# Moving the elu's positive part to the ScalarE and layer 3's bias to the heads' results in a four-layer graph attention kernel

## The chip, the cores and the metric

The kernel runs on one core of one Trainium2 chip. A core has a matrix engine (TensorE, in the profile PE; its weight loads are a row of their own, PEld), a vector engine (VectorE, DVE), an engine for activation functions (ScalarE, ACT), a general engine (GpSimd, POOL) and a queue for transfers (SyncE, SP). Each engine works through its own list of instructions in order, and they wait for each other through semaphores. The metric is the device time of one launch in microseconds (us). Before the change it is 3154.01 us, the median of 3 runs (3153.35 to 3154.1).

## The reference

The input is `x`, 16 graphs of 1024 nodes with 256 features, and `adj`, their adjacency. Four layers follow, each in the same frame: a layer norm and a relu, then a graph attention whose result is added to `x`.

```python
# --- layers 1 and 2: an elu follows the attention ---
h = jnp.maximum(_layernorm(x, axis=-1), 0.0)
x = x + _L1_gnn_ref(h, adj, ...)        # ... return jax.nn.elu(h_prime)
# (layer 0 has no elu; layer 2 is like layer 1 with other scores)

# --- layer 3: four heads of 64 features, a bias, a relu, a layer norm for each head ---
h = jnp.einsum('bnd,hde->bhne', nodes_embed, W)
# ... weight, leaky_relu, softmax -> attention
dst = jnp.einsum('bhij,bhje->bhie', attention, h) + bias[None, :, None, :]
out = jax.nn.relu(dst) + h
mu = out.mean(axis=-1, keepdims=True)
var = out.var(axis=-1, keepdims=True)
out = (out - mu) / jnp.sqrt(var + EPS) * ln_gamma[...] + ln_beta[...]
```

Two identities matter here. The elu is `max(v, 0) + min(exp(v), 1) - 1`; the kernel collects the two `-1` of layers 1 and 2 in a constant that is added with `beta`. And since the attention weights of a row sum to one, a bias may be added to the values before the attention or to its result after it.

## The kernel before

The kernel is written in a tile framework. The framework sets the semaphores and also decides, from the program's text, the order in which the instructions stand in each engine's list. Two graphs at a time are worked on as two interleaved streams, each with its own two PSUM accumulators (`acc0`, `acc1`).

The projection of a pair of node tiles, and the eviction of it in layer 3:

```python
    def project(b, l, xb, pair, evict):
        # ... bn_stats / bn_aggr per tile (DVE), rstd by pow (POOL), centered = max(x - mean, 0) (DVE)
        turned = psum.tile([P, NK, 2 * P], F32, name="misc")
        # ... four transposes on PE
        hT = wide.tile([P, NK, 2 * P], F32, name="hT", bufs=3)
        nc.scalar.copy(hT, turned)
        for n in range(2):
            projected = accumulator(b)[:, : D + EXT[l]]
            for k in range(NK):
                nc.tensor.matmul(projected, hT[:, k, ts(n, P)], W[l][:, k, :], ...)
            evict(2 * pair + n, projected, rstd[:, n : n + 1])

            def evict3(i, projected, rstd):
                nc.scalar.activation(ex[:, i, :], projected[:, D:], AF.Exp, scale=rstd)
                nc.scalar.mul(h3[:, i, :], projected[:, :D], rstd)

                q = ex[:, i, :H].unsqueeze(2)
                values = V3[:, i, :, :E]
                nc.gpsimd.tensor_add(
                    values, h3[:, i, :].rearrange("p (h e) -> p h e", h=H),
                    bias.rearrange("p (h e) -> p h e", h=H),
                )
                nc.gpsimd.tensor_mul(values, values, q.to_broadcast([P, H, E]))
                nc.gpsimd.tensor_copy(V3[:, i, :, E:], q)
                nc.gpsimd.tensor_add(xb[:, i, :], xb[:, i, :], beta)
```

The attention of layers 0 to 2: eight matmuls for each of eight node tiles, then the finish of the tile, which for layers 1 and 2 is the elu. The next layer's projection of a pair starts when both its tiles are finished.

```python
    def add_elu(xi, acc):
        inv = small.tile([P, 1], F32, name="inv")
        inverse(inv, acc[:, D : D + 1])               # max with a tiny number, reciprocal: two DVE instructions
        below = work.tile([P, D], F32, name="below", bufs=2)
        nc.scalar.activation(below, acc[:, :D], AF.Exp, scale=inv)
        above = work.tile([P, D], F32, name="above", bufs=2)
        nc.vector.tensor_scalar(above, acc[:, :D], inv, 0.0, op0=ALU.mult, op1=ALU.max)
        nc.vector.scalar_tensor_tensor(above, below, 1.0, above, op0=ALU.min, op1=ALU.add)
        nc.gpsimd.tensor_add(xi, xi, above)

            for i in range(NI):
                # ... eight matmuls into acc
                finish(i, acc)
                if l == 2:
                    next(testing)                     # one ACT pass (Square) over a tile of adj
```

Layer 3's heads: the scaled results of a head are collected in `y`, centred and scaled.

```python
        def center(h):
            yh = y[:, :, h, :]
            head = ts(h, E)
            nc.vector.scalar_tensor_tensor(yh, yh, 0.0, h3[:, :, head], op0=ALU.max, op1=ALU.add)
            mean = small.tile([P, NI], F32, name="mean")
            nc.vector.tensor_reduce(mean, yh, AX.X, ALU.add)
            nc.vector.tensor_scalar_mul(mean, mean, 1.0 / E)
            nc.vector.tensor_sub(yh, yh, mean.unsqueeze(2).to_broadcast(shape))
            # ... square (ACT), var (DVE), rstd by pow (POOL)

        def rescale(yh, head, rstd):
            nc.vector.tensor_mul(yh, yh, rstd.unsqueeze(2).to_broadcast(shape))
            nc.gpsimd.tensor_mul(yh, yh, gamma[:, head].unsqueeze(1).to_broadcast(shape))
            nc.gpsimd.tensor_add(yh, yh, xb[:, :, head])
```

## Time and profile before

| what | before |
|---|---|
| time, median of 3 runs | 3154.01 us |
| span of the profiled execution | 3152.2 us |
| PE busy | 3005.1 us (95%) |
| DVE busy | 2377.5 us (75%) |
| POOL busy | 1077.7 us (34%) |
| ACT busy | 732.0 us (23%) |
| mean granted clock of TensorE | 0.987 of full |

The page gives the busy time of each engine and, in its fourth part, the chain of work that ended last: starting at the last instruction, it goes back from each instruction to the one that released it. An engine can be busy most of the time and still not set the end; the chain tells which one does. The groups of instructions give, for one source line, how many there were, how long one took, and how long the engine stood idle just before them. The waits list the same idle times by who waited for whom. The timeline lists instructions in order of time, which is needed where the question is what happens at one place in the program; the pattern repeats about every 383 us, once for each pair of graphs.

### The profile page before, as it was taken

To read this page: it belongs to the slowest core of one execution; us is meant where nothing else is said; L and a number is where in the kernel's file an instruction comes from. 1 tells how busy PE (TensorE), PEld (TensorE's weight loads), DVE (VectorE), ACT (ScalarE), POOL (GpSimd) and SP (SyncE) were. 2 spreads that over 40 slices of the span, in tenths; PEclk is the share of its full clock that TensorE was granted. 3 is DMA by queue.
4 is the path that set the end of the run, shared out by engine and by line. 5 is a ranking of instruction groups with operands and counts; after the bars stand their busy time and mean duration, and the time that the engine had idled before them with its cause. 6 is when DMAs were issued, how large, how long until landed. Compare 5 with 4: busy or idle time off the path is not lost.

```text
span 3152.2 us, 35624 instructions
## 1 busy us (share of the span) xinstructions
PE 3005.1 (95%) x12678; PEld 2071.0 (66%) x12678; DVE 2377.5 (75%) x5243; ACT 732.0 (23%) x1729; POOL 1077.7 (34%) x1460
## 2 busy tenths in 40 slices
PE   7899999999999999999999999999999999999987
PEld 5676766668666686666767567666775657766662
DVE  5677678786878768787687876878768787787756
ACT  1221223113131221312213122231222212222130
POOL 1332424233252342423425224252333423233242
PEclk9999999999999999999999999999999999999998
DMA  5512212122120221302303022021221221001010
GB/s 112 65 16 27 47 21 43 25 27 51 17 61 7 54 29 13 64 4 54 41 2 66 8 54 34 14 54 14 51 30 21 47 27 40 14 14 27 1 28 15
DMA packets 116872, 105.53 MB, mean 33 GB/s; under 512 B 73680, under 2 KB 91216, under 8 KB 116688
## 3 DMA queue, kind: packets, MB, share of 16 engines
q0 software_dynamic: 44256, 81.80, 15.9%
q1 hardware_dynamic: 72432, 21.37, 3.6%
q8 instruction: 103, 1.69, 0.2%
q14 instruction: 81, 0.66, 0.1%
HBM read 153.49 MB, written 33.55 MB: 59 GB/s over the span
## 4 chain that ended last, share of the span: by engine, by line
PE 81%; DVE 10%; POOL 4%; ACT 2%; issue 1%; DMA 1%; ACTq 0%; POOLq 0%; SPq 0%; DVEq 0%
PE acc L383 36%; PE acc L489 27%; PE acc L271 12%; DVE weights L292 5%; PE misc L264 3%; PE row L288 2%; POOL rstd L239 1%; PE misc L504 1%; DVE stats L251 1%; DVE above L317 1%; ACT below L315 1%; POOL out_dram L520 1%; POOL x_b L319 1%; DMA weights<-in_L_gnn_a_src_dram 1%; DVE centered L256 1%
## 5 line engine op out<-in xcount | busy, mean ns | idle before, releaser
L383 PE MATMUL acc<-V,weights 128*128 128x257 f32 x6144 | 1435.2, 383 | 23.1 <-DVE weights L292 11.0
L383 PEld LDWEIGHTS acc<-V,weights 128*128 128x128 f32 x6144 | 1149.2, 191 | 325.2 <-issue 90.3
L489 PE MATMUL acc<-weights,V 128*65 128x512 f32 x2048 | 957.9, 592 | 1.5 <-POOL V L358 1.5
L239 POOL TENSOR_TENSOR rstd<-rstd,minus_half 128x2 f32<-128x2 f32 (+1 forms) x320 | 295.2, 924 | 1054.0 <-DVE rstd L238 1040.8
L292 DVE SCALAR_TENSOR_TENSOR weights<-row,ex,mask 128x1024 f32<-128x1024 f32 x512 | 626.9, 1275 | 18.7 <-PE acc L489 9.3
L271 PE MATMUL acc<-W,hT 128*128 128x259 f32 (+1 forms) x2048 | 536.9, 401 | 59.4 <-DVE above L317 25.6
L271 PEld LDWEIGHTS acc<-W,hT 128*128 128x128 f32 x2048 | 389.8, 197 | 195.8 <-issue 70.8
L292 DVE SCALAR_TENSOR_TENSOR weights<-row,V,mask 128x1024 f32<-128x1024 f32 x384 | 475.1, 1275 | 45.7 <-PE row L288 45.7
L489 PEld LDWEIGHTS acc<-weights,V 128*65 128x65 f32 x2048 | 272.7, 138 | 353.5 <-issue 313.5
L319 POOL TENSOR_TENSOR x_b<-x_b,above 128x256 f32<-128x256 f32 x256 | 188.2, 738 | 687.6 <-DVE above L318 609.5
L315 ACT ACTIVATE below<-acc,inv 128x256 f32<-128x256 f32 x256 | 120.6, 473 | 821.3 <-DVE inv L308 571.3
L251 DVE BATCH_NORM_STATS2 stats<-x_b 128x6 f32<-128x256 f32 x512 | 209.1, 415 | 109.6 <-POOL x_b L319 101.5
L266 ACT COPY hT<-misc 128x512 f32<-128x512 f32 x256 | 149.5, 585 | 476.8 <-PE misc L264 476.3
L256 DVE TENSOR_SCALAR centered<-x_b,mv 128x256 f32<-128x256 f32 x512 | 216.6, 425 | 4.6
L264 PE MATMUL misc<-ident,centered 128*128 128x128 f32 x1024 | 166.8, 278 | 37.9 <-DVE centered L256 28.7
L264 PEld LDWEIGHTS misc<-ident,centered 128*128 128x128 f32 x1024 | 127.0, 142 | 114.9 <-DVE centered L256 48.4
L333 ACT ACTIVATE V<-acc,rstd 128x3 f32<-128x3 f32 x384 | 98.9, 262 | 423.7 <-PE acc L271 422.1
L337 DVE TENSOR_SCALAR V<-acc,rstd,V 128x256 f32<-128x256 f32 x256 | 134.5, 538 | 75.0 <-ACT V L333 73.4
L317 DVE TENSOR_SCALAR above<-acc,inv 128x256 f32<-128x256 f32 x256 | 122.2, 480 | 69.2 <-ACT below L315 68.7
L499 ACT COPY sums<-acc 65x512 f32<-65x512 f32 x128 | 74.5, 582 | 378.8 <-PE acc L489 378.8
L307 DVE TENSOR_SCALAR inv<-acc 128x1 f32<-128x1 f32 x256 | 39.2, 153 | 146.1 <-PE acc L383 143.9
L132 ACT ACTIVATE adj_i<-adj_i,minus_half 128x1024 bf16<-128x1024 bf16 x128 | 145.8, 1139 | 0.0
(68 smaller groups left out, 1946.7 us busy)
## 6 DMA issues: line engine op xcount, KB each, us to landing
adj_i<-in_adj_dram POOLq DMA_DIRECT2D x128, 256.0 KB, 3.9
narrow<-in_adj_dram POOLq DMA_DIRECT2D x64, 256.0 KB, 8.8
out_dram<-y POOLq DMA_DIRECT2D x32, 512.0 KB, 4.0
x_b<-in_x_dram POOLq DMA_DIRECT2D x14, 1024.0 KB, 7.1
x_b<-in_x_dram SPq DMA_DIRECT2D x2, 1024.0 KB, 7.4
mask<-narrow SPq DMA_TRANSPOSE x64, 3.8
W<-in_L_gnn_W_dram SPq DMA_DIRECT2D x3, 256.0 KB, 11.4
weights<-in_L_gnn_a_dram SPq DMA_DIRECT2D x3, 256.0 KB, 12.8
```

The costliest lines, as they stand in the source:

```text
L239: nc.gpsimd.tensor_tensor(r, r, minus_half.to_broadcast([P, n]), op=ALU.pow)
L251: nc.vector.bn_stats(stats, xb[:, 2 * pair + n, :])
L256: nc.vector.tensor_scalar(centered[:, n, :], xb[:, 2 * pair + n, :], mv[:, n, 0:1], 0.0, op0=ALU.subtract, op1=ALU.max,)
L264: nc.tensor.transpose(turned[:, k, ts(n, P)], centered[:, n, ts(k, P)], ident)
L266: nc.scalar.copy(hT, turned)
L271: nc.tensor.matmul(projected, hT[:, k, ts(n, P)], W[l][:, k, :], start=(k == 0), stop=(k == NK - 1),)
L292: nc.vector.scalar_tensor_tensor(w, r, c(j), masks[b][:, j // 2, :, j % 2], op0=op, op1=ALU.mult)
L315: nc.scalar.activation(below, acc[:, :D], AF.Exp, scale=inv)
L317: nc.vector.tensor_scalar(above, acc[:, :D], inv, 0.0, op0=ALU.mult, op1=ALU.max)
L319: nc.gpsimd.tensor_add(xi, xi, above)
L383: nc.tensor.matmul(accs[i], weights[j][:, ts(i, P)], V[:, j, : D + 1], start=(j == 0), stop=(j == NI - 1),)
L489: nc.tensor.matmul(accT, V3[:, j, h, :], weights[h * NI + j][:, ts(g, HALF)], start=(j == 0), stop=(j == NI - 1),)
```

## The change

The change has two parts. In `add_elu` the positive part of the elu is computed by ACT, as a relu of the accumulator scaled by `inv`, right after the exponential of the same accumulator, and no longer by DVE. This takes an instruction from the busier of the two engines that read the accumulator. In layer 3 the bias is no longer added to the values in `evict3`, where it cost one addition for each node tile; it is added to a head's results at the start of `center`, one addition for each head over all eight node tiles. Both additions stand on POOL.

```diff
         below = work.tile([P, D], F32, name="below", bufs=2)
         nc.scalar.activation(below, acc[:, :D], AF.Exp, scale=inv)
         above = work.tile([P, D], F32, name="above", bufs=2)
-        nc.vector.tensor_scalar(above, acc[:, :D], inv, 0.0, op0=ALU.mult, op1=ALU.max)
+        nc.scalar.activation(above, acc[:, :D], AF.Relu, scale=inv)
         nc.vector.scalar_tensor_tensor(above, below, 1.0, above, op0=ALU.min, op1=ALU.add)
         nc.gpsimd.tensor_add(xi, xi, above)
@@
                 nc.scalar.mul(h3[:, i, :], projected[:, :D], rstd)
-
                 q = ex[:, i, :H].unsqueeze(2)
-                values = V3[:, i, :, :E]
-                nc.gpsimd.tensor_add(
-                    values, h3[:, i, :].rearrange("p (h e) -> p h e", h=H),
-                    bias.rearrange("p (h e) -> p h e", h=H),
-                )
-                nc.gpsimd.tensor_mul(values, values, q.to_broadcast([P, H, E]))
+                nc.gpsimd.tensor_mul(
+                    V3[:, i, :, :E], h3[:, i, :].rearrange("p (h e) -> p h e", h=H),
+                    q.to_broadcast([P, H, E]),
+                )
                 nc.gpsimd.tensor_copy(V3[:, i, :, E:], q)
@@
             yh = y[:, :, h, :]
             head = ts(h, E)
+            nc.gpsimd.tensor_add(yh, yh, bias[:, head].unsqueeze(1).to_broadcast(shape))
             nc.vector.scalar_tensor_tensor(yh, yh, 0.0, h3[:, :, head], op0=ALU.max, op1=ALU.add)
```

## The prediction

> **What bounds the kernel now.** I read the busy shares first, then the chain of work that ended last, then the groups, to see what the change touches. These are lines of the page:

> ```profile
> PE 3005.1 (95%) x12678; PEld 2071.0 (66%) x12678; DVE 2377.5 (75%) x5243; ACT 732.0 (23%) x1729; POOL 1077.7 (34%) x1460
> ...
> PE 81%; DVE 10%; POOL 4%; ACT 2%; issue 1%; DMA 1%; ACTq 0%; POOLq 0%; SPq 0%; DVEq 0%
> ```

> PE is busy for 95% of the span and carries 81% of the chain. The change adds no matmul and takes none away. So it can only move the time in which PE stands still or runs slowly. How much is that? I took the busy time by stretches, without the first 300 us and the end:

> ```profile
> 300.00:3000.00 2700.00, 2624.31 (x11136) 1813.19 (x11135) 2072.71 (x4551) 641.36 (x1518) 938.68 (x1267) 0.99 0.18 31
> ```

> In these 2700 us PE is idle for 75.7 us. If all of it went, the kernel would be 2.4% faster; that is about the ceiling, and the change touches a small share of it. Next, the groups that the change removes, copies or delays:

> ```profile
> L317 DVE TENSOR_SCALAR above<-acc,inv 128x256 f32<-128x256 f32 x256 | 122.2, 480 | 69.2 <-ACT below L315 68.7
> L315 ACT ACTIVATE below<-acc,inv 128x256 f32<-128x256 f32 x256 | 120.6, 473 | 821.3 <-DVE inv L308 571.3 <-PE acc L383 149.7 <-DVE inv L307 57.2
> ...
> L358 POOL TENSOR_TENSOR V<-h,bias 128x256 f32<-128x256 f32 x128 | 93.6, 732 | 2.5 <-ACT h L354 2.1
> L463 POOL TENSOR_TENSOR y<-y,gamma 128x512 f32<-128x512 f32 x64 | 81.5, 1274 | 74.2 <-DVE inv L308 36.8 <-DVE y L462 25.2 <-DVE inv L307 6.4
> ```

> And from the waits, those in which PE stands behind the elu or behind the next layer's input:

> ```profile
> PE misc L264 <- DVE centered L256: 28.7, 27, 3.4
> PE acc L271 <- DVE above L317: 25.6, 12, 2.9
> ...
> PE acc L383 <- DVE above L317: 7.7, 17, 1.2
> ```

> So PE waits 33.3 us in all for an accumulator that the positive part still reads. The largest of these waits is 2.9 us and comes back in every period of 383 us. The timeline of one shows where it comes from:

> ```profile
> 930.02 1.55 POOL L520 DMA_DIRECT2D out_dram<-y  x2 [0.30 <-POOL y L464]
> ...
> 931.59 0.73 POOL L319 TENSOR_TENSOR x_b<-x_b,above 128x256 f32<-128x256 f32 x1
> ...
> 932.36 0.43 DVE L251 BATCH_NORM_STATS2 stats<-x_b 128x6 f32<-128x256 f32 x1 [0.53 <-POOL x_b L319]
> ...
> 933.49 0.16 DVE L308 RECIPROCAL inv<-inv 128x1 f32<-128x1 f32 x1
> ...
> 933.77 0.47 ACT L315 ACTIVATE below<-acc,inv 128x256 f32<-128x256 f32 x1 [2.92 <-DVE inv L308]
> ...
> 934.28 0.48 DVE L317 TENSOR_SCALAR above<-acc,inv 128x256 f32<-128x256 f32 x1 [0.62 <-ACT below L315]
> ...
> 934.91 0.51 PE L271 MATMUL acc<-W,hT 128*128 128x268 f32 x1 [2.89 <-DVE above L317]
> ```

> The name in the last bracket is the positive part, but the chain behind it starts on POOL: the issue of the finished graph's store, then the sum of the previous elu, then the statistics that stand ahead of this tile's `inv` in DVE's list. Right after the stall the stretch 935 to 939 us has a granted clock of 0.57, its neighbours 1.00. So such a stall costs more than its 2.9 us: at about half speed, four microseconds lose some 1.7 us more.

> [...]the positive part starts at 934.28, just after the exponential of the same accumulator ends at 934.24, and 68.7 us of DVE idle time is put down to that. [...]the trace before has one table load, of 1.3 us.[...]

> **The change part by part.**
> 1. Removed from DVE: 256 x 480 ns = 122 us, and with it the 69 us of waiting for the exponential. DVE falls to about 2255 us (72%). But its next instruction, the sum of the two parts, now waits for ACT instead.
> 2. Added on ACT: 256 x 473 ns = 121 us, 853 us (27%) in all. It stands directly after the exponential, ahead of the square over `adj` that follows each elu of layer 2.
> 3. Release of the accumulator. Before: exponential at 933.77, positive part over at 934.76, thus 0.99 us. After: two ACT passes of 0.473 us, 0.95 us. Each release gains 0.05 us, and more where DVE's list was late for it. Of the 33.3 us, seven stalls of 2.9 us (20.2 us) hang on the POOL chain and stay; of the remaining 13 us I expect 5 us to go.
> 4. What waits behind ACT: a copy of `hT` queued after an elu comes 0.47 us later. PE waits 24.5 us for `hT` in 32 places; I put +2 us.
> 5. Layer 3's values: 128 additions of 732 ns leave POOL, 93.6 us. A node tile's values are ready 0.73 us earlier; PE waits only once for them (1.5 us, line 489), so this is worth 0.7 us.
> 6. Layer 3's results: 64 additions over 128x512 come onto POOL. The product with gamma has the same shape and the same kind of broadcast, 1274 ns: 81.5 us. POOL ends at about 1066 us, the same.
> 7. These additions stand between two DVE instructions: the scaled results, then relu plus `h3`. In the changed program's order the second follows the first at once or after one or two others, so DVE stands for up to 1.27 us plus about 0.12 us of hops, 1.4 us. 64 x 1.4 = 90 us of DVE idle at most, which about takes back what part 1 gave. Inside a head PE does not feel it: its matmuls there wait 1.5 us in all. At the two layer boundaries of each period, where the last head of one graph falls together with the other graph's projections, some of it comes through: 14 x 0.3 us = 4 us.
> 8. At those boundaries POOL is relieved of two additions of 0.73 us. DVE instructions run longer beside POOL there (the subtraction of line 454 takes up to 1769 ns against a median of 693), so I count -2 us, and another -2 us for the waits for `centered`, from the freed DVE.
> 9. The end: the last head has nothing beside it, so its addition adds 1.4 us to the span.

> Sum: -5 + 2 - 0.7 + 4 - 2 - 2 + 1.4 = -2.3 us. I choose 3151 us.

> **The rivals.** First, the freed DVE could matter more: the order of the lists also changes, on PE by about a tenth of its rows, and at one boundary the changed program puts matmuls of the attention between projections that stood alone before. If that fills the 2.9 us stall, its half clock goes too: 7 x 4.6 = 32 us, thus 3120 us. For it: the stall is a matter of order. Against it: its chain runs over POOL's store and the statistics, which stand there in the changed order too. Second, the wait of DVE for POOL could become the bound at the boundaries: 14 x 1.4 us plus some new half clocks, 20 to 35 us, thus 3175 to 3190 us. For it: DVE is busy almost without a gap there. Against it: at one such place POOL is idle for 3.1 us just when the new addition becomes ready, and would do it in that gap. Third, ACT in the chain (a square of 1.14 us ahead of an exponential) could delay releases: the matmuls of two node tiles take 7.5 us (16 x 2 passes x 0.234 us, line 383's busy time by its count), and ACT then has about 6.6 us for them (two elus 1.9, two squares with their read-out 2.7, one `hT` 0.6, two evictions 1.5). It fits, but not by much; I hold this for the weakest, as before the change it was 5.7 us and ACT was not in the chain.

> **Range and chances.** The small terms each have an error of their own size, some 5 us together; the change of order is the larger unknown, of some 15 to 20 us either way. So 8 in 10 lie between 3124 and 3172 us. 2% is 63 us and would need more than four fifths of PE's idle time to vanish, or as much to appear: faster 0.015, within 2% 0.97, slower 0.015.

> **What would show it.** DVE busy near 2255, ACT near 853, POOL near 1066 us; the relu at about 473 ns; PE busy the same within 10 us and its idle time in 300 to 3000 us between 60 and 95 us; the stall of about 2.9 us once in a period still there, ended by the relu; the sum behind the bias addition waiting for POOL for about 1 us, 64 times. The prediction is wrong if the granted clock shows more or fewer dips than one in each period, or if a new wait on PE names the bias addition.

## The result, and the profile after

| | device time, us | range | granted clock, profiled execution |
|---|---|---|---|
| before | 3154.06 | 3153.35 to 3155.75 | 0.987 |
| after | 3172.74 | 3171.57 to 3174.14 | 0.985 |

The changed kernel takes 1.0059 times as long, with a 95% interval of 1.0046 to 1.0071: 18.7 us slower. Predicted were 3151 us, 3124 to 3172. So the time lies just above the range, and on the other side of the kernel before.

The page of the changed kernel has these two lines for the busy shares and for the chain that ended last:

```profile
PE 3014.2 (95%) x12678; PEld 2067.3 (65%) x12678; DVE 2282.1 (72%) x4987; ACT 817.1 (26%) x1985; POOL 1074.1 (34%) x1396
...
PE 62%; DVE 22%; POOL 8%; ACT 4%; issue 3%; DMA 1%; ACTq 0%; POOLq 0%; SPq 0%; DVEq 0%
```

The shares are close to those that were worked out ahead. But the chain is another one: before, PE carried 81% of it, DVE and POOL 14%; now PE carries 62%, DVE and POOL 30%. The stretch from 300 to 3000 us (columns: length; busy us and instructions of PE, PEld, DVE, ACT, POOL; granted clock; DMA share; GB/s):

```profile
300.00:3000.00 2700.00, 2620.52 (x11094) 1804.72 (x11093) 1993.20 (x4320) 713.49 (x1736) 935.05 (x1209) 0.99 0.18 31
```

In the same 2700 us PE gets 42 fewer instructions done than before (11094 against 11136). It is idle for only 3.8 us more, 79.5 against 75.7. Part of the remainder is work at a lower clock, which counts as busy: in this stretch PE has half clock for 44.4 us, before for 37.5. The waits of the changed kernel (us in total, times, longest):

```profile
DVE stats L251 <- POOL x_b L319: 140.2, 155, 3.8
...
DVE above L318 <- ACT above L317: 108.9, 143, 1.3
...
DVE y L448 <- POOL y L447: 48.3, 34, 3.4
...
PE acc L271 <- ACT above L317: 31.0, 29, 2.7
PE misc L264 <- DVE centered L256: 26.1, 26, 3.5
...
PE acc L271 <- ACT hT L266: 17.9, 26, 0.7
```

And two of the same waits in the kernel before:

```profile
DVE stats L251 <- POOL x_b L319: 101.5, 135, 2.4
...
PE acc L271 <- ACT hT L266: 24.5, 32, 1.1
```

Line 448 is relu plus `h3`, line 447 the new bias addition. DVE waits for it 34 times, for up to 3.4 us, not for about 1 us 64 times. The wait of the statistics for POOL's sum grew from 101.5 to 140.2 us. By the experiments below this growth comes with the relu and not with the bias addition (101.8 us in e2, 128.0 in e1), and it is no cost by itself: a2, which is faster, has 145.2. The groups of the elu and of the new addition, first the sum of the elu's two parts as it was before:

```profile
L318 DVE SCALAR_TENSOR_TENSOR above<-below,above 128x256 f32<-128x256 f32 x256 | 114.2, 451 | 3.8
```

```profile
L318 DVE SCALAR_TENSOR_TENSOR above<-below,above 128x256 f32<-128x256 f32 x256 | 129.6, 506 | 109.0 <-ACT above L317 108.9
...
L317 ACT ACTIVATE above<-acc,inv 128x256 f32<-128x256 f32 x256 | 120.2, 470 | 0.0
...
L447 POOL TENSOR_TENSOR y<-y,bias 128x512 f32<-128x512 f32 x64 | 83.9, 1311 | 404.0 <-DVE y L505 344.4 <-DVE rstd L238 43.7 <-DVE inv L307 9.8
```

The sum of the two parts of the elu (line 318) reads and writes what it did before, and takes 506 ns where it took 451.

**Where the time went.** A period, two graphs, took 383.34 us before and 385.51 after (mean of six, measured between the same attention matmuls). That is 6 x 2.17 = 13.0 us. The time from the last head's last matmul to the end grew from 22.5 to 27.9 us, 5.4 more. The start and the last graphs differ by another 0.7. Together that is 19.1 us; the spans of the two profiles, 3152.2 and 3171.4, differ by 19.2.

I read each period further with the list of granted clocks. PE had half clock for 4.55 us of a period before and for 6.26 us after. Two matmuls of a projection (line 271, 259 columns) that follow each other at once start 432 ns apart at half clock and 219 ns at full, by the medians of both profiles. So half of the time at half clock counts as lost, 0.85 us of the 2.17. PE's idle time grew by 0.80 us, from 10.59 to 11.39. The remaining half microsecond is busy time that neither of the two explains.

These are two single executions, and the clock differs from one execution to the next: in 109 executions of the kernel before, its mean lies between 0.983 and 0.988. One less the mean clock, times the span, is what the clock would cost if PE were busy throughout; I call it the nominal loss. On average it is 44.3 us in these 109 and 46.1 us in the 11 executions of the changed kernel. The difference of 1.8 us is no more than the longer end gives: behind PE's last instruction, where PE has nothing left to do, half clock lasts 18.9 us before and 22.7 after in the two profiles, and half of these counts in the nominal loss. So the clock does not carry the 18.7 us; the two profiles put too much on it.

The tail can be read directly from the timeline of the changed kernel (start, length, engine, line):

```profile
3137.10 1.27 POOL L461 TENSOR_TENSOR y<-y,gamma 128x512 f32<-128x512 f32 x1 [4.97 <-DVE inv L308]
3137.14 0.42 DVE L505 TENSOR_TENSOR y<-misc,inv 128x256 f32<-128x256 f32 x1
...
3138.45 1.26 POOL L462 TENSOR_TENSOR y<-y,x_b 128x512 f32<-128x512 f32 x1
...
3139.67 1.26 POOL L447 TENSOR_TENSOR y<-y,bias 128x512 f32<-128x512 f32 x1
...
3140.97 0.69 DVE L448 SCALAR_TENSOR_TENSOR y<-y,h 128x512 f32<-128x512 f32 x1 [3.40 <-POOL y L447]
```

The results of this head are ready at 3137.56. POOL has just begun the previous head's product with gamma, and its sum with x stands next in the list. The bias addition is third, so DVE waits 3.4 us for 1.3 us of work. For the last head it is 2.6 us again.

### The profile page after: what moved, and what is told of

Read it like the earlier page. It is cut to its first block, busy times and chain, and to the rows that moved or that the text cites. A ratio compares the mean times of both kernels' runs of the same rounds, so it can differ in the third digit from the quotient of the medians.

```text
span 3171.4 us, 35608 instructions
## 1 busy us (share of the span) xinstructions
PE 3014.2 (95%) x12678; PEld 2067.3 (65%) x12678; DVE 2282.1 (72%) x4987; ACT 817.1 (26%) x1985; POOL 1074.1 (34%) x1396
## 4 chain that ended last, share of the span: by engine, by line
PE 62%; DVE 22%; POOL 8%; ACT 4%; issue 3%; DMA 1%; ACTq 0%; POOLq 0%; SPq 0%; DVEq 0%
PE acc L380 29%; PE acc L487 18%; DVE weights L292 10%; PE acc L271 10%; PE misc L264 2%; DVE stats L251 2%; DVE centered L256 2%; POOL rstd L239 2%; POOL x_b L319 2%; PE row L288 2%; POOL y L447 1%; DVE above L318 1%; POOL y L462 1%; POOL y L461 1%; ACT above L317 1%
## 5 line engine op out<-in xcount | busy, mean ns | idle before, releaser
L292 DVE SCALAR_TENSOR_TENSOR weights<-row,ex,mask 128x1024 f32<-128x1024 f32 x512 | 627.3, 1274 | 15.0 <-PE row L288 8.9
L271 PE MATMUL acc<-W,hT 128*128 128x259 f32 (+1 forms) x2048 | 536.5, 400 | 62.0 <-ACT above L317 31.0
L271 PEld LDWEIGHTS acc<-W,hT 128*128 128x128 f32 x2048 | 387.7, 196 | 201.6 <-ACT above L317 53.6
L319 POOL TENSOR_TENSOR x_b<-x_b,above 128x256 f32<-128x256 f32 x256 | 189.1, 739 | 727.7 <-DVE above L318 698.1
L315 ACT ACTIVATE below<-acc,inv 128x256 f32<-128x256 f32 x256 | 121.4, 474 | 831.6 <-DVE inv L308 534.5
L251 DVE BATCH_NORM_STATS2 stats<-x_b 128x6 f32<-128x256 f32 x512 | 208.3, 417 | 148.7 <-POOL x_b L319 140.2
L256 DVE TENSOR_SCALAR centered<-x_b,mv 128x256 f32<-128x256 f32 x512 | 225.5, 444 | 5.1
L447 POOL TENSOR_TENSOR y<-y,bias 128x512 f32<-128x512 f32 x64 | 83.9, 1311 | 404.0 <-DVE y L505 344.4
L318 DVE SCALAR_TENSOR_TENSOR above<-below,above 128x256 f32<-128x256 f32 x256 | 129.6, 506 | 109.0 <-ACT above L317 108.9
L264 PEld LDWEIGHTS misc<-ident,centered 128*128 128x128 f32 x1024 | 127.9, 144 | 105.0 <-issue 45.0
L264 PE MATMUL misc<-ident,centered 128*128 128x128 f32 x1024 | 163.4, 280 | 34.7 <-DVE centered L256 26.1
L307 DVE TENSOR_SCALAR inv<-acc 128x1 f32<-128x1 f32 x256 | 39.5, 154 | 150.9 <-PE acc L380 148.4
```

The costliest lines, as they stand in the source:

```text
L251: nc.vector.bn_stats(stats, xb[:, 2 * pair + n, :])
L256: nc.vector.tensor_scalar(centered[:, n, :], xb[:, 2 * pair + n, :], mv[:, n, 0:1], 0.0, op0=ALU.subtract, op1=ALU.max,)
L264: nc.tensor.transpose(turned[:, k, ts(n, P)], centered[:, n, ts(k, P)], ident)
L292: nc.vector.scalar_tensor_tensor(w, r, c(j), masks[b][:, j // 2, :, j % 2], op0=op, op1=ALU.mult)
```

## The experiments

Three theories stood at the start. A: the relu puts ACT into the chain that releases accumulators. B: the bias addition on POOL, between two DVE instructions, lengthens the chain at the layer boundaries. C: neither; the scheduler merely orders the lists differently. Each kernel ran beside the kernel before on the same chip, whose median there was 3157 to 3160 us; so the ratios are compared, not the times. 0.1% is 3.2 us. "Lost" is half of the time at half clock in a period; "rest" is the period less that loss; "end" is the time from the start of the last head's last matmul. These columns come from one profile each, and so "lost" and "rest" are to be read with the averages over all executions that the text gives beside them.

| kernel | us | ratio to before, 95% | period | lost | rest | end |
|---|---|---|---|---|---|---|
| before | 3154.06 | 1 | 383.34 | 2.28 | 381.06 | 22.5 |
| after | 3172.74 | 1.0059 (1.0046-1.0071) | 385.51 | 3.13 | 382.38 | 27.9 |
| e1 relu only | 3161.51 | 1.0010 (1.0003-1.0016) | 384.96 | 3.13 | 381.83 | 22.7 |
| e2 bias only | 3160.59 | 1.0008 (1.0000-1.0017) | 383.06 | 1.42 | 381.64 | 27.9 |
| e3 relu, no bias | 3142.63 | 0.9950 (0.9937-0.9964) | 382.51 | 2.28 | 380.23 | 23.0 |
| e4 DVE, no bias | 3145.46 | 0.9960 (0.9946-0.9973) | 381.80 | 1.71 | 380.10 | 22.5 |
| a0 after again | 3174.03 | 1.0051 (1.0037-1.0064) | 385.75 | 3.41 | 382.34 | 27.9 |
| a1 bias ahead | 3211.86 | 1.0170 (1.0156-1.0185) | 390.73 | 4.27 | 386.46 | 26.1 |
| a2 bias on DVE | 3153.47 | 0.9984 (0.9975-0.9993) | 382.27 | 0.57 | 381.70 | 25.4 |
| a3 relu twice | 3200.96 | 1.0142 (1.0126-1.0159) | 388.04 | 3.13 | 384.92 | 27.9 |
| b1 relu in layer 1 | 3159.94 | 1.0006 (0.9997-1.0014) | 382.83 | 1.42 | 381.41 | 28.2 |
| b2 relu in layer 2 | 3172.58 | 1.0051 (1.0037-1.0065) | 385.40 | 2.84 | 382.55 | 28.4 |
| b3 after, other store queue | 3154.96 | 0.9991 (0.9984-0.9998) | 383.31 | 1.99 | 381.32 | 25.7 |
| b4 bias fused | 3123.13 | 0.9894 (0.9879-0.9909) | 378.92 | 0.85 | 378.07 | 21.4 |
| c1 after, short square | 3172.82 | 1.0048 (1.0035-1.0062) | 385.63 | 3.41 | 382.22 | 27.9 |
| c2 before, short square | 3145.83 | 0.9965 (0.9951-0.9979) | 381.37 | 2.28 | 379.10 | 22.5 |
| c3 before, other store queue | 3142.57 | 0.9954 (0.9940-0.9968) | 381.21 | 1.14 | 380.07 | 20.3 |
| c4 relu, bias fused | 3118.65 | 0.9874 (0.9859-0.9889) | 379.08 | 0.57 | 378.51 | 21.4 |
| d1 after, filled | 3177.31 | 1.0061 (1.0047-1.0075) | 385.64 | 1.42 | 384.22 | 27.9 |
| d2 before, filled | 3153.87 | 0.9986 (0.9977-0.9994) | 383.60 | 1.14 | 382.46 | 22.4 |

### The two parts alone

```diff
 # e1: before, with
-        nc.vector.tensor_scalar(above, acc[:, :D], inv, 0.0, op0=ALU.mult, op1=ALU.max)
+        nc.scalar.activation(above, acc[:, :D], AF.Relu, scale=inv)
 # e2: before, with the values' addition gone and, in center(),
+            nc.gpsimd.tensor_add(yh, yh, bias[:, head].unsqueeze(1).to_broadcast(shape))
```

> The kernel before, with the relu on ACT as the only change; layer 3's bias stays in the values. Theory A (ACT's list is what holds PE: the relu stands ahead of the evictions that give accumulators and transposed inputs back, and PE now waits for ACT at places where it did not): this part alone costs most of the 18.7 us, so 3167 to 3173 us, and the waits of PE that name ACT are as long as in the changed kernel. Theory B (the bias addition between two DVE instructions holds DVE at the layer boundaries): no loss, 3146 to 3156 us. Theory C (neither duration matters, only the order of the lists, which any edit reshuffles): anything within 20 us of 3154, not adding up with the other part.

> The kernel before, with layer 3's bias moved to the heads' results as the only change; the positive part stays on DVE. Theory A: 3152 to 3158 us. Theory B: most of the loss, 3167 to 3173 us, with DVE waiting for POOL's bias addition in some 34 places for about 48 us as in the changed kernel. Theory C: within 20 us of 3154, and the two parts' differences do not add up to 18.7 us.

Measured: +0.10% and +0.08%. Theories A and B each expected one part to carry most of the loss. Neither part explains +0.59%, and their sum doesn't. In the profiles the rests add up (+0.77 and +0.58 make 1.35 us, and the change has +1.32) and the clock losses don't (+0.85 and -0.86, and together +0.85). The averages over all executions don't bear this out. Against the kernel before on the same chip the nominal loss is 2.6 us larger in e1, 4.6 smaller in e2 and 0.6 larger in the changed kernel (a0 below). That leaves 2.6 us of the 10 us by which the times fail to add up. The parts alone aren't halves of the changed kernel in their waits either: the stall at the boundary is 4.36 us in e1, beside a second one of 2.20 us in each period, 2.59 in e2 and 2.65 with both.

### No bias addition at all

These two leave layer 3's bias out altogether; their output lacks it.

```diff
 # e3: after, without
-            nc.gpsimd.tensor_add(yh, yh, bias[:, head].unsqueeze(1).to_broadcast(shape))
 # e4: before, with
-                nc.gpsimd.tensor_add(values, h3..., bias...)
-                nc.gpsimd.tensor_mul(values, values, q.to_broadcast([P, H, E]))
+                nc.gpsimd.tensor_mul(values, h3..., q.to_broadcast([P, H, E]))
```

> The changed kernel without the bias addition on the heads' results; the bias of layer 3 is left out altogether. Theory A: the loss stays, 3164 to 3172 us. Theory B: the loss goes, 3145 to 3156 us. Theory C: no rule, within 20 us of 3154.

> The kernel before without any addition of layer 3's bias (left out altogether), positive part on DVE. It removes 93.6 us of POOL work and adds none. Theory A and B: 3148 to 3154 us, since POOL is not the bound and PE waits 1.5 us in all for those values. Theory C: this pure removal moves the time by several us up or down too.

In e4 the instructions of PE, DVE and ACT stand in exactly the order of the kernel before; only POOL's 128 additions are gone. That is worth 0.40%, 12.6 us. I had counted them as off the path. Likewise e3 has the order of e1 on those three engines, and is 0.60% below it, 19 us. So additions on POOL cost time though POOL is busy for only 34% of the span.

Against the same base the additions to the results cost 0.48% without the relu (e2 against e4, 15 us) and 1.01% with it (a0 against e3, 32 us). The additions to the values cost 13 and 19. The relu alone changes the time by -0.10% (no bias; the intervals of e3 and e4 overlap), +0.10% (bias in the values), +0.43% (bias in the results).

### Where the addition stands, and on which engine

```diff
 # a1: after; POOL's list: bias addition of head h ahead of gamma and x of head h-1
+                nc.gpsimd.tensor_add(yh, yh, bias[:, ts(h, E)]...)
                 if h > 0:
                     rescale(*normed.pop())   # its product with gamma pinned behind the addition
 # a2: after, with
-            nc.gpsimd.tensor_add(yh, yh, bias[:, head]...)
+            nc.vector.tensor_add(yh, yh, bias[:, head]...)
```

> The changed kernel once more, beside the next three on one chip, because relu alone (+0.10%) and bias alone (+0.08%) did not add up to its +0.59%. If the parts are additive and the rest was the difference between chips or days: ratio about 1.002 to 1.003 (+6 to +9 us). If the two parts really work on each other: again 1.005 to 1.007 (+16 to +22 us).

> The changed kernel with one change of order: on POOL each head's bias addition now stands ahead of the previous head's product with gamma and sum with x (gamma is pinned behind it). Theory B (the addition waits behind 2.5 us of POOL work of the previous head, and DVE waits with it): the waits of the DVE line after it fall from 48 us to about 15 us, the tail after the last head's matmuls loses 2.5 to 3.5 of its 5.4 us, and the whole is 3 to 6 us faster than the changed kernel. Theory A (ACT's list holds PE up): the whole stays within 3 us of it. The order on the other engines changes as well, which may move some us either way.

> The changed kernel with the bias addition of the heads' results on DVE in place of POOL: 64 additions of about 0.69 us between two DVE instructions, no hop to another engine, no queue. Theory B: the tail falls from 22.4 + 5.4 us to about 22.4 + 1.4 us (two heads at 0.7 us), POOL's chain at the boundaries is as short as without a bias, DVE busy 44 us more; in all 6 to 14 us faster than the changed kernel. Theory A: only the tail's 4 us; the period stays at about 385.5 us.

a0 repeats +0.5%: the parts do work on each other.

a1 missed by far. It does shorten the end by 1.8 us, and the longest wait for the addition from 3.4 to 1.7 us. Yet it is 1.2% slower than a0, though PE's and ACT's lists are the same and three DVE instructions have moved. The timeline of a0 and that of a1 at the same place show why:

```profile
1472.00 1.27 POOL L447 TENSOR_TENSOR y<-y,bias 128x512 f32<-128x512 f32 x1
...
1473.30 0.69 DVE L448 SCALAR_TENSOR_TENSOR y<-y,h 128x512 f32<-128x512 f32 x1 [1.38 <-POOL y L447]
...
1474.02 0.69 DVE L450 TENSOR_REDUCE mean<-y 128x8 f32<-128x512 f32 x1
...
1476.98 1.36 PE L271 MATMUL acc<-W,hT 128*128 128x259 f32 x5 [0.72 <-ACT hT L266]
```

```profile
1487.59 1.26 POOL L512 TENSOR_TENSOR y<-y,bias 128x512 f32<-128x512 f32 x1
1488.81 1.27 POOL L460 TENSOR_TENSOR y<-y,gamma 128x512 f32<-128x512 f32 x1
...
1488.89 1.74 DVE L447 SCALAR_TENSOR_TENSOR y<-y,h 128x512 f32<-128x512 f32 x1 [1.38 <-POOL y L512]
...
1490.66 0.69 DVE L449 TENSOR_REDUCE mean<-y 128x8 f32<-128x512 f32 x1
...
1493.86 0.92 PE L271 MATMUL acc<-W,hT 128*128 128x259 f32 x3 [1.99 <-ACT hT L266]
```

Up to the addition both run alike. In a1 POOL goes straight on to the product with gamma, just when DVE's next instruction starts. That instruction takes 1.74 us in place of 0.69 and ends at 1490.63, 0.55 us after POOL's product. The 1.05 us pass down DVE's list, and PE waits 1.27 us longer. Over all heads the instruction takes 1367 ns in a1 and 754 in the changed kernel, 64 x 0.61 = 39 us more, and a1 is 38 us slower; from 300 to 3000 us PE is idle for 104.6 us in a1 and 79.1 in a0. The eight longest of the elu's sums in the changed kernel lie beside POOL's work too: they take 1.37 to 1.41 us, where the median is 0.43, and each overlaps a bias addition. Why a DVE instruction takes longer there was not shown.

In a2 the addition is 0.71 us on DVE, with nothing to wait for:

```profile
L448 DVE SCALAR_TENSOR_TENSOR y<-y,h 128x512 f32<-128x512 f32 x64 | 46.8, 731 | 0.9
...
L447 DVE TENSOR_TENSOR y<-y,bias 128x512 f32<-128x512 f32 x64 | 45.5, 712 | 0.7
```

DVE gets 45 us of work and loses 48 us of waiting. All the same a2 is 0.67% faster than a0, 21 us, and 0.16% faster than before. It is more than I gave theory B. By the table, the rest falls by 0.64 us a period and the clock loss from 3.41 to 0.57. Averaged over all executions the nominal loss falls from 46.3 to 34.9 us, which is about half of the gain.

```diff
 # a3: after, with the relu written twice
         nc.scalar.activation(above, acc[:, :D], AF.Relu, scale=inv)
+        nc.scalar.activation(above, acc[:, :D], AF.Relu, scale=inv)
```

> The changed kernel with the relu written twice in a row into the same tile: ACT gets 256 more passes of about 0.37 to 0.47 us and each accumulator is held that much longer. Theory A: each release that PE waits for comes 0.37 us later; with some 60 such waits and the hT copies behind them 20 to 35 us slower than the changed kernel, and PE's waits on lines that ACT ends (accumulator and hT) about double. Theory B or C (bias addition, or order of the lists only): under 8 us slower, waits on ACT up by less than 8 us.

27 us slower than a0, as theory A said. PE's wait for `hT` rises from 17.9 to 57.6 us. So ACT time does count here once there is more of it; the order of the lists changed as well.

### The relu, layer by layer

```diff
 # b1 (b2 with l == 2): after, with
-        nc.scalar.activation(above, acc[:, :D], AF.Relu, scale=inv)
+        if l == 1:
+            nc.scalar.activation(above, acc[:, :D], AF.Relu, scale=inv)
+        else:
+            nc.vector.tensor_scalar(above, acc[:, :D], inv, 0.0, op0=ALU.mult, op1=ALU.max)
```

> The changed kernel, but only the elu of layer 1 has its relu on ACT; that of layer 2 has its positive part on DVE again, as before the change. With the bias on the heads' results, relu in both layers costs about 13 us over relu in none (3174 against 3160.6). Theory A1 (relu costs ACT time wherever PE waits for an accumulator): half of it, 3166 to 3168. Theory A2 (it costs where layer 2's elu stands with the other graph's head and the squares over adj on ACT, and the order of the lists changes there: 340 of 7568 PE instructions move with layer 2, 76 with layer 1): most of the 13 us is gone, 3158 to 3163.

> The counterpart: relu on ACT only in layer 2, positive part on DVE in layer 1, bias on the heads' results as in the changed kernel. Theory A1: 3166 to 3168 as well. Theory A2: nearly the whole cost, 3170 to 3175.

This is clear. In layer 1 the relu costs nothing (1.0006 against e2's 1.0008). Layer 2 has the whole cost (1.0051). In the profiles much of it is clock. Below are consecutive clock windows after the boundary stall, first of a0, then of b1. The columns are as in the stretch above; the granted clock is the third from the right.

```profile
1705.20:1708.61 3.41, 1.17 (x4) 0.68 (x4) 2.08 (x7) 0.49 (x2) 3.37 (x6) 1.00 0.67 256
1708.61:1712.02 3.41, 2.46 (x7) 1.91 (x8) 1.51 (x5) 3.25 (x9) 2.70 (x5) 0.50 0.76 269
1712.02:1715.44 3.42, 3.42 (x11) 2.84 (x10) 0.54 (x1) 1.21 (x3) 2.64 (x6) 0.50 1.05 222
1715.44:1718.85 3.41, 3.41 (x17) 2.94 (x17) 1.50 (x4) 0.79 (x3) 0.00 (x0) 1.00 0.12 23
```

```profile
1698.22:1701.63 3.41, 1.28 (x5) 0.82 (x5) 2.29 (x9) 0.79 (x4) 3.39 (x5) 0.99 0.81 308
1701.63:1705.04 3.41, 2.88 (x7) 2.27 (x8) 2.31 (x6) 2.64 (x7) 3.36 (x8) 0.50 0.78 225
1705.04:1708.46 3.42, 3.42 (x17) 2.77 (x17) 1.31 (x3) 1.11 (x3) 2.07 (x4) 1.00 1.03 231
```

The stall itself is almost equal, 2.65 and 2.59 us. In the window of the stall PE is busy for 1.17 of 3.41 us (34%) and 1.28 (38%); both are followed by half clock. In the half window PE is busy for 72% in a0 and 84% in b1. Only a0 gets a second half window. In 300 to 3000 us, a0 has 47.8 us at half clock and b1 17.1; half of the difference is 15 us, and b1 is 0.45% faster, 14 us. But the stretch leaves out the start and the end, and over all executions the nominal loss is 46.3 us in a0, 45.0 in b2 and 39.3 in b1: 6 to 7 us, or about half of the cost at most.

### The store, out of POOL's list

```diff
 # b3: after, c3: before, each with
-            nc.gpsimd.dma_start(
+            nc.sync.dma_start(
                 in_blocks(out[b, ts(g, HALF), :]),
```

> The changed kernel with the two stores of the finished graph issued from SyncE's queue in place of POOL's: 1.55 us leave POOL's list just where the sum of the previous elu waits behind them (the chain of the 2.65-us stall); the lists of PE and ACT stay as they are, two DVE instructions move. Theory B (POOL's in-order list is in the chain at the boundary): the stall falls from 2.65 to about 1.1 us and its half clock shortens or goes, 7 times 1.5 to 3.5 us, thus 10 to 25 us faster than the changed kernel. Theory A (ACT is the bound there): the stall keeps more than 2 us, the whole within 4 us.

> The kernel before with only the stores moved from POOL's queue to SyncE's; the lists of PE, DVE and ACT stay exactly as they are. The same move made the changed kernel 19 us faster. If the POOL chain sets the stall of 2.9 us in both kernels: stall down to about 1.4 us, its half clock shorter or gone, 10 to 20 us faster. If the gain belonged to the changed kernel's longer half clock alone: 3 to 8 us.

0.60% and 0.46% faster: 19 and 15 us. In c3 the other three engines have exactly the lists of before. The sum behind the store starts earlier; the statistics wait for POOL 92.0 us in c3 where it was 101.5. The stall shrinks by less than the 1.55 us that left POOL (2.88 to 2.28 us in most periods of c3, 2.65 to 1.94 at 1702 us of b3). The timeline of b3 shows why:

```profile
1698.26 0.84 POOL L121 DMA_DIRECT2D x_b<-in_x_dram  x1 [0.30 <-POOL y L462]
...
1699.13 0.73 POOL L319 TENSOR_TENSOR x_b<-x_b,above 128x256 f32<-128x256 f32 x1
...
1702.28 2.16 PE L271 MATMUL acc<-W,hT 128*128 128x268 f32 x4 [1.94 <-ACT above L317]
```

In the place of the store's issue, 1.54 us in a0, the issue of a load of the next input (line 121, 0.84 us) now stands ahead of the sum. So POOL's list gains 0.70 us there, and the stall ends 0.70 us earlier. In c3 the load takes 0.90 us, the list gains 0.65, and the stall is 0.60 us shorter. So POOL's in-order list is in the chain that ends the stall in both kernels.

### ACT's square cut short

```diff
 # c1: after, c2: before; seven eighths of the test over adj are left out
-                adj_i, adj_i, AF.Square, bias=minus_half, accum_out=...
+                adj_i[:, :P], adj_i[:, :P], AF.Square, bias=minus_half, accum_out=...
```

> The changed kernel with the square over adj on ACT cut to 128 of its 1024 columns (seven eighths of that test are left out; its loads stay). In the changed kernel exponential, relu, square (1.15 us) and two small exponentials stand ahead of the copy of hT just before the 2.65-us stall; PE waits 0.7 us for that copy, and the stretch at half clock is 6.8 us in place of 3.4. Theory A2 (relu's cost in layer 2 is ACT time in front of hT and h, which lengthens the half clock): without the square that wait goes, half clock in 300 to 3000 us falls from 45 to under 30 us, and the time falls by 9 to 15 us, to about 3160. Theory C (only the order of the lists): less than 5 us faster.

> The kernel before with the same cut of the square, as the control: there the copy of hT waits behind an exponential and a square only. Theory A2: 0 to 5 us faster than before, as ACT is not in the chain of its stall. If ACT's square were a cost in both kernels alike, 9 to 15 us here too.

A miss on both sides: the changed kernel gains nothing (1.0048), and the control gains 0.35%, 11 us. The waits of c1:

```profile
PE acc L271 <- ACT above L317: 36.5, 29, 3.4
...
PE acc L271 <- ACT hT L266: 12.8, 19, 0.7
```

The wait of 0.7 us ahead of the stall did go, but the stall grew by the same, 2.65 to 3.38 us. What ends it comes along POOL and DVE, and an earlier `hT` only makes PE wait longer there. The half clock stayed as it was. So c1 speaks against ACT's time in front of `hT` as the reason why the relu costs in layer 2. Why the control gains 11 us stays open. Another difference shows in the two timelines. From the start of the last head's bias addition to the matmul that ends the stall it takes 18.84 us in a0 and 17.51 in b1. In a0 four statistics and two subtractions of the other graph stand between line 448 and line 456 in DVE's list, with a wait for POOL of 0.62 us among them. From the start of 448 to the end of 456 it takes 5.98 us. In b1 two statistics and two evictions stand there, and it takes 4.73. That is order, theory C; it wasn't run alone and isn't shown.

### The bias without POOL

```diff
 # b4: before, without the values' addition, stores from SyncE's queue, and
-            nc.vector.tensor_mul(y[:, ts(g, NG), h, :], acc[:, :, :E], inv...)
+            for i in range(NG):
+                nc.vector.scalar_tensor_tensor(y[:, g * NG + i, h, :], acc[:, i, :E],
+                    inv[:, i : i + 1], bias[:, ts(h, E)], op0=ALU.mult, op1=ALU.add)
 # c4: the same with the relu on ACT
```

> The positive part on DVE as before the change, the bias fused into the scaling of the heads' results on DVE (per 128 nodes: scaled by inv and bias added in one instruction, four of 64 columns in place of one of 256), so that POOL adds no bias at all; stores from SyncE's queue. POOL loses 94 us and the 1.55 us at each boundary; DVE gains 128 times 3 instructions of some 0.15 us, about 60 us. Theory B (what POOL does at the boundary sets the stalls, directly and by making DVE's instructions longer): at least the 13 us of the kernel without a bias and more for the store, 3130 to 3145. Theory A or C (DVE's and ACT's lists set them): DVE's extra instructions at the boundary cost as much, 3155 to 3165.

> The best kernel so far (bias fused into the scaling on DVE, stores from SyncE's queue: 3123 us) with the relu on ACT in both layers as in the changed kernel. If relu's cost needs POOL's addition and store beside it (their stall, whose half clock it lengthens): 3119 to 3126, relu then neither costs nor gains. If relu costs by itself: 3132 to 3140. If DVE is now what bounds the boundaries, relu on ACT gains there: 3105 to 3118.

Both compute everything, and both beat the two kernels: 0.9894 and 0.9874, 3118.65 us for c4. The page of c4:

```profile
PE 2991.0 (96%) x12678; PEld 2062.9 (66%) x12678; DVE 2294.1 (74%) x5371; ACT 821.2 (26%) x1985; POOL 981.8 (31%) x1300
...
PE 74%; DVE 13%; POOL 5%; issue 4%; ACT 3%; SPq 1%; DMA 1%; ACTq 0%; POOLq 0%; DVEq 0%
```

DVE's scaling takes 113.7 us in c4, 512 instructions of 277 ns, where 128 of 419 ns took 53.6 us before. PE's busy time is 23 us below that of the changed kernel with the same 12678 instructions. By the two profiles the clock goes with 14 of them: in 300 to 3000 us c4 has 17.1 us at half clock where the changed kernel has 44.4, and half of the difference is lost time. The relu costs nothing here: the intervals of b4 and c4 overlap. It costs nothing in e3 against e4 either, where no bias is added and the stores are still issued by POOL. So its cost is not its own, and it doesn't need the stores: it appears with the additions to the results on POOL. In each of these kernels the lists of PE and DVE are ordered otherwise too, so that the additions do it without the order isn't shown.

### Filling the stall

```diff
 # d1: after, d2: before; ahead of the second tile of one projection in each period
+            if l == 3 and b % 2 == 0 and b >= 2 and pair == 1 and n == 1:
+                for f in range(14):
+                    nc.tensor.transpose(turned[:, 0, :P], centered[:, 0, :P], ident)   # pinned
```

> The changed kernel with 14 useless transposes of 0.109 us (1.5 us, results not read) put on PE into the wait of 2.65 us, once in each period. They lengthen no chain as long as they fit into the wait. Clock theory (a clock window of 3.41 us in which PE is busy for less than about half is followed by windows at half clock, and these are 3.4 us lost in each period of 385.7): the dips at the seven stalls go, half clock in 300 to 3000 us falls from 45 us to under 12, 15 to 24 us faster than the changed kernel, 3149 to 3158. If the half clock were only a reading of the trace, or hung on the longest wait elsewhere: within 4 us of it.

> The same 14 transposes at the same place in the kernel before, whose stall is 2.9 us. Its half clock costs 2.3 us in a period of 383.3 by the profile: 10 to 16 us faster than before, 3141 to 3148. The changed kernel so filled should then stand 8 to 14 us above this one: that is the part of the change's cost that is not clock (the tail's 5.4 us and about 1.3 us of waits in each period).

Both missed: d1 is 0.10% slower than a0 where 15 to 24 us of gain were expected, and d2 is 0.14% faster than the kernel before, 4 us in place of 10 to 16. They are inconclusive. For the clock theory: in the changed kernel from 300 to 3000 us, PE was busy for 0.25 to 0.44 of each of the seven windows of 3.41 us ahead of a half clock, and for 0.55 or more of every other window at full clock. The half clock did fall (47.8 to 20.5 us in d1 from 300 to 3000 us), and by the profile the loss by 2.0 us a period. But the rest grew by 1.9, and in d2 the loss fell by 1.1 and the rest grew by 1.4. Behind the transposes PE's list had another matmul than before, one that waits for an `hT` behind ACT's square (2.34 us). The fill changed the order, so these two don't show what the clock alone is worth.

## Why the prediction failed

By its own steps:

- **1, DVE's load.** 2282 us in place of 2255: the elu's sum got longer, 256 x 55 ns = 14 us (470 ns with the relu alone in e1, 506 with the additions on POOL beside it, 451 before). The wait of 69 us wasn't removed, it became 109 us of waiting for ACT. Harmless, as the step said.
- **2, ACT's load.** 817 in place of 853 us, with one table load of 1.3 us as before. The relu takes 470 ns, but it starts 0.37 us after the exponential; the two overlap by 0.1 us.
- **3, the accumulator.** The mechanism was right: the seven stalls stayed (2.65 us after 2.88), with the relu as the last name. The 5 us of gain didn't come: PE waits 33.9 us for the elu where it was 33.3. The half clock behind the stall, which the step took as given, grew from 4.55 to 6.26 us a period in the profiles, but hardly on average.
- **4, hT behind ACT.** Wrong in sign, small: 17.9 us in place of 24.5.
- **5 and 8, the values' additions leave POOL.** Put at -0.7 us and, for the relief at the boundaries, -2 us. Removing them alone, with the other engines' lists unchanged, gave -12.6 us. This term was mis-sized by about a factor of five.
- **6, the additions' work.** Right: 1311 ns each and POOL at 1074 us.
- **7 and 9, DVE behind the addition, and the tail. This is the step that failed.** It put "up to 1.27 us plus about 0.12 us of hops" on each addition, let 0.3 of it through at 14 boundaries, and 1.4 us at the end: 5.4 us. The hop was sized well where POOL is free (1.38 us at 1473). But POOL's list is in order, and at the end the addition stands behind two instructions of the head before, so the wait is 3.4 us and the end 5.4 us longer. At the boundaries DVE's instructions beside it take longer (the elu's sum 1.37 to 1.41 us, against a median of 0.43). The runs put the additions to the results at 15 us without the relu, and 32 with it.

The two large terms stand against each other, -13 and +15. The prediction had them at about -3 and +5, so it saw their net as small for the wrong reason. Without the relu the net was even right, +2.7 us predicted and +2.5 measured (e2), and that was luck. On top comes what it had no term for at all: beside the relu the same additions cost some 17 us more (32 against 15), and with the bias in the results all that the relu costs comes with layer 2. With the relu's own -3 us (e3 against e4) the sum is -3 - 13 + 15 + 17 = +16 us, the +0.51% of a0. Of the 14 us by which the relu raises the time with the bias in the results, the average clock goes with 6 to 7.

Of the rivals, the second (DVE waiting for POOL at the boundaries, with new half clocks: 3175 to 3190) came closest to 3172.7. The third (ACT) is spoken against by c1, and supported only where ACT got still more to do, in a3. The first (the order fills the stall) didn't happen.

What stays open: why the relu in layer 2 costs time beside the additions (without the clock a period of b2 is 0.9 us longer than one of e2, 382.55 and 381.64 in their profiles). The order of DVE's list is the best candidate by the timelines, not shown. And how much of the 14 us the half clock causes, rather than accompanies. A hint: in the kernel before, 10 executions with a clock of 0.984 have a mean span of 3160.9 us and 12 with 0.988 one of 3153.0. That is 7.9 us for 12.6 us of nominal loss, so that an estimate from this would be about 4 of the 14 us.

## What to carry to other kernels

An engine that is busy for only a third of the time (POOL, 34% here) isn't free. An instruction put on its list between two instructions of another engine can cost the queue ahead of it (3.4 us of wait for 1.3 us of work at the end) and longer instructions beside it (1.74 us in place of 0.69 in a1), and not only its own duration; read the list around it before counting. Take such work off the boundary first (fused bias, stores on another queue: 1.1 to 1.3% here), and only then judge which engine should do the relu, for its effect went from nothing to 0.43% with what POOL did beside it. And don't split a difference into clock and waits by one profile of each kernel: the averages over all executions gave another split.

## What the hardware showed

Stalls of nearly the same length were followed by different stretches. Of the seven of 2.88 to 2.89 us in the kernel before, four were followed by one window at half clock and three by two; of the seven of 2.65 to 2.66 us in the changed kernel, one by one window and six by two. In a2, with a longest such stall of 2.7 us, the half clock is 2 x 0.57 = 1.14 us a period by the table, two windows in the six periods. In the changed kernel the last six stalls are 385.5 to 385.9 us apart, about 113 windows, and begin at 0.55 to 0.65 of a window. In the kernel before they are 382.8 to 384.2 us apart and begin anywhere from 0.07 to 1.00 of one.
